# Graph attention on one core: keys fetched in three parts, query blocks stored in two parts, rows in two buffers

## The chip, the cores and the metric

The kernel runs on 1 core of a Trainium2 chip. The metric is device microseconds of one execution; a profiled execution gives the trace from which all rows below come. The five engines are named as in the profile: PE (TensorE), DVE (VectorE), ACT (ScalarE), POOL (GpSimd) and SP (SyncE, which here does nothing but issue transfers). "SPq" is SP's own queue of instructions, worked off strictly in order.

## What is computed

One layer of graph attention with five relation types, on 3125 nodes of 128 features and 100000 edges that are sorted by destination.

```python
def _fused_forward(node_embeddings, W_Q, W_K, W_V, attn_bias, out_proj_w, out_proj_b, ln_gamma, ln_beta, edge_index, edge_types):
    src, dst = (edge_index[0], edge_index[1])
    x_src = node_embeddings[src]
    x_dst = node_embeddings[dst]
    for r in range(R):                                   # 5 relations, 8 heads of 16
        mask = edge_types == r
        q = jnp.einsum('eh,khd->ekd', x_dst, W_Q[r])
        k = jnp.einsum('eh,khd->ekd', x_src, W_K[r])
        v = jnp.einsum('eh,khd->ekd', x_src, W_V[r])
        logits = (q * k).sum(-1) / scale + attn_bias[r][None, :]
        ... softmax over the edges of one destination, relation and head ...
        out = out + jax.ops.segment_sum(attn[:, :, None] * v, dst, num_segments=n)
    out = out.reshape(n, HIDDEN) @ out_proj_w.T + out_proj_b
    h = out + node_embeddings
    ... layer norm with ln_gamma, ln_beta ...
x = _layernorm(x + _L0_gnn_ref(x, edge_index, edge_type_5, ...), axis=-1)
```

## The kernel before

**Tiles and steps.** The 100000 edges are cut into 196 groups (`NGR`) of 512 (`GE`), each of four tiles (`T`) of 128 edges; 782 tiles (`NTILE`) hold edges. A step handles three groups (`G3`); `STEPS` puts the one left over into the first step, so there are 66 steps (`NST`): one of one group and 65 of three.

**Preamble.** For each of 25 blocks of 128 nodes, `table` (L472) multiplies the turned block with all key and value weights and stores a table row per node and relation in HBM, `kv_d` (L488). Between the blocks, the dictionary `side` (L650) places small pieces of work: loading indices, `keys_a/b/c`, `begins` (L404), masks, checks that the input has the expected form. `begins` takes the first destination of every tile from `fr`, which was loaded from HBM one element at a time, and makes from it `first`, `first15` (the row in `q_d` at which a tile's queries begin) and `gap`; `lr` holds the last destination of every group, loaded in the same way. On POOL, 60 gathers (`EARLY`, L355) fetch source rows of x into `xg` for the tiles that are treated below as early. The first four blocks' queries go to HBM as `q_d`, each query in three bf16 parts (L675).

**Gathers.** `gather(k)` (L796) fetches, on POOL, one tile per indirect transfer (L801) from `kv_d` into one of four slots of step k, three steps ahead of its use (`AHEAD`). A step in the steady part has 12 tiles; for 60 steps (`early_at`) one of them is not gathered but computed on PE from `xg` (`early_turn` L976, `early_rows` L985).

**What SP issues.** `fetch_rows(k)` (L712) loads for each of the step's 12 tiles the 120 query rows that its edges can need: for every four tiles one register load (L687), and for each tile one transfer of 30 KB from `q_d` (L717). `fetch_keys(k)` (L698) loads the step's keys, broadcast to 120 partitions, as one transfer of 360 KB. `fetch_masks(k)` (L846, transfer L850) loads the segment masks for the scans, `store_z` (L1222) stores finished output blocks. `store_q` (L842, transfer L675) stores one block of queries, 480 KB, into `q_d`; a block comes every third step or so, made in two halves in successive steps (`queries`, `first_part`, `remainder`, `second_part`, `third_part`). A transfer that reads `q_d` waits on SP until the last store into `q_d` has landed, and a store into `q_d` waits until the row loads issued before it have landed.

**The loop** (L1270), written out by hand; the order on each engine is the order of the calls. In step k: `products` and `logits` (query times key, summed by head, DVE), `turn_logits` (PE), `norm` and `relations` of step k-2, `spread_q(k+1)` (PE: one-hot times rows puts the right query beside each edge), `third_part` and `store_q`, `weigh(k-1)`, `gather(k+3)`, the two `scans` (DVE, L1002 and L1005: segment maxima both ways, they need the mask), `less_max`, `exps`, `spot(k+2)` (DVE: one-hot from the keys, L707), `turn_exps`, node-block work, and at the end:

```python
    def take(k):                                          # L1258
        if k + 3 < NST:
            fetch_keys(k + 3)
            fetch_rows(k + 3)
        if k + 2 < NST:
            fetch_masks(k + 2)
```

The keys have one buffer (`bufs=1`, so the transfer of step k+3 waits for `spot(k+2)`), the rows three, the masks two. After the loop, L1371 to L1406 finish the last three node blocks (`begun` and the two after it).

Of the kernel before, what the change touches and what calls it, by code (L numbers as in the profile page):

```python
# [9 lines left out]
F32 = mybir.dt.float32  # L10
BF16 = mybir.dt.bfloat16
# [36 lines left out]
STEPS = [NGR % G3] + [G3] * (NGR // G3)  # L48
# [21 lines left out]
ROUND, OFROUND, ROUNDS = 21, 20, 3  # L70
# [70 lines left out]
def windowed_path(  # L141
# [15 lines left out]
    def keep(name, shape, dt=F32):  # L157
        return const.tile(shape, dt, name=name)
# [6 lines left out]
    first15 = keep("first15", [1, NGR * T], I32)  # L165
# [40 lines left out]
    fr = load.tile([1, NGR * T], I32, name="fr")  # L206
    nc.vector.memset(fr[:, NTILE:], 0)
# [12 lines left out]

    early_src = load_early(nc.sync, "early_src", src)
# [49 lines left out]
    lr = load.tile([1, NGR], I32, name="lr")  # L271

    with nc.allow_non_contiguous_dma(reason="one element of each group"):
        for t, n, step, at in ((fr, NTILE, P, 0), (lr, NGR - 1, GE, GE - 1)):
            nc.scalar.dma_start(
                t[:, :n],
                bass.AP(tensor=dst.tensor, offset=dst.offset + at, ap=[[step * n, 1], [step, n], [1, 1]]),
            )
# [10 lines left out]
    nc.sync.dma_start(lr[:, NGR - 1 :], dst[E - 1 : E].rearrange("(o g) -> o g", o=1))  # L289
# [61 lines left out]
    busy(6)  # L351
    nc.vector.tensor_copy(xi, early_turned_up("early_src", early_src))
    busy(12)
    for e in range(EARLY):
        nc.gpsimd.indirect_dma_start(  # L355
            out=xg[:, e, :], out_offset=None, in_=x[:, :],
            in_offset=bass.IndirectOffsetOnAxis(ap=xi[:, e : e + 1], axis=0),
        )
# [45 lines left out]
    def begins():  # L404
        nc.vector.tensor_copy(frf, fr[:, ::T])
        nc.vector.tensor_copy(first, fr[:, ::T])
        nc.vector.tensor_scalar_mul(first15, fr, float(R * 3))
        fp = pps.tile([P, NGR], F32, name="fp", tag="tr", bufs=2)
        nc.tensor.matmul(fp, ones[0:1, :], frf, start=True, stop=True)
        firsts = load.tile([P, NGR], F32, name="firsts")  # L410
        nc.vector.tensor_copy(firsts, fp)
# [177 lines left out]
    lrf = load.tile([1, 2, NGR], F32, name="lrf")  # L589

    def wide_ends():
        nc.vector.tensor_copy(lrf[:, 0, :], lr)
# [20 lines left out]
    def short_tiles():  # L613
        spans = load.tile([HG, 2, T], F32, name="spans")
        nc.vector.tensor_tensor(
            spans, dst_r[:, :, P - 1 :: P], dst_r[:, :, ::P], op=ALU.subtract
        )
        nc.vector.tensor_scalar(
            spans, spans, float(QN - 1), None, op0=ALU.is_gt, op1=ALU.add,
            accum_out=vio[:HG, 6:7],  # L620
        )
        last = load.tile([1, 1], F32, name="last")
        nc.vector.tensor_tensor(
            last, lr[:, NGR - 1 :], fr[:, NTILE - 1 : NTILE], op=ALU.subtract
        )
        nc.vector.tensor_scalar(
            vio[0:1, 7:8], last, float(QN - 1), None, op0=ALU.is_gt
        )
# [17 lines left out]
    def late_x():  # L646
# [14 lines left out]
        10: [lambda: along(kvrow, 1, put_idx), begins],  # L661
        11: [keys_b],
        12: [sorted_rows, short_tiles],
# [22 lines left out]
    def starts(table, a, b, engine):  # L686
        _, at = nc.values_load_multi_w_load_instructions(  # L687
            table[0:1, a:b],
            engines=[engine],
            min_val=0,  # L690
            max_val=(N - 1) * (R * 3 if table is first15 else 1),
            skip_runtime_bounds_check_because="destinations are nodes",
        )
        return at
# [3 lines left out]
    def fetch_keys(k):  # L698
        n = B0[k + 1] - B0[k]
        live["kt", k] = kt = ahead.tile([3 * QR, TB * P], BF16, name="kt", bufs=1)  # L700
        keys = key_d.rearrange("g e -> (g e)")[B0[k] * P : B0[k + 1] * P]
        nc.sync.dma_start(kt[:, : n * P], keys.partition_broadcast(3 * QR))
# [9 lines left out]
    def fetch_rows(k):  # L712
        live["qw", k] = qw = ahead.tile([3 * QR, TB, H], BF16, name="qw", bufs=3)
        for a in range(B0[k], B0[k + 1], T):
            b = min(a + T, B0[k + 1])
            for j, f in enumerate(starts(first15, a, b, SPE)):
                nc.sync.dma_start(qw[:, a + j - B0[k], :], q_d[bass.ds(f, 3 * QR), :])  # L717
# [124 lines left out]
    def store_q(b):  # L842
        live.pop(("xT", b))
        store_rows(b, live.pop(("q3", b)))
# [82 lines left out]
    def closed_lanes(k):  # L927
        n, lg, lx = len(groups(k)), live.pop(("lg", k)), live["lx", k]
        into = lx.rearrange("p (u j) r k -> p j u r k", u=T)
        a, m = max(B0[k], 1), lg.shape[1]  # L930
        if m == T * n:
            closed(into[:, 1 : n + 1], lg, a)
        else:
            closed(into[:, 1:n], lg[:, : T * (n - 1)], a)
            closed(into[:, n : n + 1, : T - 1], lg[:, T * (n - 1) :], a + T * (n - 1))
            nc.vector.memset(lx[:SEG, (T - 1) * (G3 + 1) + n], 0.0)
# [297 lines left out]
    begun = max(b for b in range(NT) if done_at[b] < NST)  # L1234
    block_at = {k: b for b, k in done_at.items() if b < begun}
# [20 lines left out]
    fetch_rows(2)  # L1256

    def take(k):  # L1258
        if k + 3 < NST:
            fetch_keys(k + 3)  # L1260
            fetch_rows(k + 3)
        if k + 2 < NST:
            fetch_masks(k + 2)
# [6 lines left out]
    for k in range(NST):  # L1270
        new, old = k >= 1, k >= 2
        q0, (q, c0, c1), (q1, d0, _) = q_at.get(k), half(k), half(k - 1)
# [19 lines left out]
        if k == NST - 2:  # L1292
            places(G0[k + 1])
        elif k == NST - 1:
            place_next()
            place_g.append(G0[k] + 1)
# [14 lines left out]
        if q1 is not None:  # L1311
            third_part(q1, d0)
            if d0:
                store_q(q1)
# [10 lines left out]
        if k == NST - 1:  # L1325
            place_next()
        sum_next()
        scans(k)
        if k == done_at[begun]:
            project(begun)  # L1330
# [9 lines left out]
        if k < NST - 1:  # L1340
            place_next()
        if k == NST - 1:
            places(G0[k] + 2)
# [5 lines left out]
        if k == NST - 1:  # L1349
            for b in range(NT - len(ends), NT):  # L1350
                lifted(b)
            for b in range(begun, NT):
                shifted(b)
            residual(begun)
# [10 lines left out]
        if k < NST - 1:  # L1365
            weights(k)
        take(k)
# [4 lines left out]
    rest = [begun, begun + 1, begun + 2]  # L1372
    g = list(groups(k))
    assert rest[-1] == NT - 1 and done_at[begun - 1] < k - 1 and done_at[begun] < k
    assert full_at(rest[1]) < G0[k] and len(g) == G3
# [3 lines left out]
    weights(k)  # L1379
# [7 lines left out]
    norms(begun)  # L1387
    store_z(begun - 1)
    sums(g[1])
    project(rest[1])  # L1390
    residual(rest[1])
    roots(rest[1], last=True)
    sums(g[2])
    norm(k)
    relations(k, room[:, 2 * GE :])
    by_node(k)
    norms(rest[1])
    store_z(begun)
    project(rest[2])
    residual(rest[2])  # L1400
    roots(rest[2], last=True)
    norms(rest[2])
    store_z(rest[1])
    roots(NT, 1, 2, last=True)
    norms(NT)
    store_z(rest[2])  # L1406
# [507 lines left out]
```

## Time and profile before

| | |
|---|---|
| median of 3 runs | 1048.62 us (1045.79 to 1054.4) |
| profiled execution, own time | 1046.48 us |
| its span (first to last instruction) | 1044.2 us |
| busy: PE, DVE, POOL, ACT | 895.8, 883.0, 755.3, 718.6 us |
| mean granted TensorE clock | 0.922 |
| DMA | 192.83 MB, mean 185 GB/s |

The own time is 2.3 us over the span, for what lies before the first and after the last instruction. "Busy" of POOL leaves out what it needs between two gathers, and SP does not appear among the busy engines at all: issuing transfers, loading registers and waiting are not counted as busy. SP's rows are to be had from the timeline of its queue and from the table of its waits.

### The profile page before, as it was taken

What the parts mean: (1) busy time and instruction counts of PE and PEld (TensorE: products, weight loads), DVE (VectorE), ACT (ScalarE), POOL (GpSimd) and SP (SyncE); (2) the same over time, 40 slices, a digit from 0 to 9 for tenths busy, and PEclk for the clock granted to TensorE, in tenths of its full rate; (3) what the DMA queues carried; (4) which work ended last, traced back from release to release, by engine and by line L of the source; (5) the groups of instructions that cost most, each with busy time, mean ns of one, the idle gap of its engine ahead of it and who ended that gap; (6) DMA issues with size and microseconds to landing.
All of it is one profiled execution on the core that took longest, in us unless ns stands there. A gap on an engine that the chain in (4) does not pass through costs nothing.

```text
span 1044.2 us, 19181 instructions
## 1 busy us (share of the span) xinstructions
PE 895.8 (86%) x5371; PEld 660.7 (63%) x5371; DVE 883.0 (85%) x1383; ACT 718.6 (69%) x1936; POOL 755.3 (72%) x795
## 2 busy tenths in 40 slices
PE   6995589998999898889889988979989898979874
PEld 3553357776766676667667666757666666666653
DVE  2675479998998898999898998989989799979974
ACT  1444258886887677778677877768877787867562
POOL 6776777777777777777777777777777777777730
PEclk8997589998999898999899998989999899999786
DMA  6997667767677677777777777676777777767720
GB/s 157 353 331 258 172 172 185 180 179 184 175 194 190 177 191 181 187 175 182 190 180 190 191 180 174 181 187 186 187 193 180 189 182 196 176 177 179 171 64 13
DMA packets 176735, 192.83 MB, mean 185 GB/s; under 512 B 122398, under 2 KB 137640, under 8 KB 176498
## 3 DMA queue, kind: packets, MB, share of 16 engines
q0 software_dynamic: 36640, 98.65, 37.4%
q1 hardware_dynamic: 138190, 91.94, 31.9%
q10 hardware_dynamic: 1788, 0.92, 0.4%
q8 instruction: 45, 0.74, 0.3%
q14 instruction: 72, 0.59, 0.2%
HBM read 161.00 MB, written 30.40 MB: 183 GB/s over the span
## 4 chain that ended last, share of the span: by engine, by line
PE 30%; DVE 19%; DMA 13%; SPq 12%; POOL 10%; issue 9%; ACT 5%; ACTq 1%; DVEq 0%; POOLq 0%
SPq L717 8%; POOL kv_late L801 6%; PE qe L990 6%; DMA mk<-msk_d 5%; PE pr L479 5%; PE both L1075 5%; POOL kv_early L801 4%; SPq L687 4%; DVE lt L1002 4%; DVE lt L1005 3%; PE lt L979 3%; PE mid L1027 3%; DMA kv_early<-kv_d,idx 2%; DVE lg L921 2%; DMA q_d<-q 2%
## 5 line engine op out<-in xcount | busy, mean ns | idle before, releaser
L801 POOL DMA_INDIRECT kv_early<-kv_d,idx x368 | 353.9, 962 | 117.7 <-issue 105.4
L801 POOL DMA_INDIRECT kv_late<-kv_d,idx x354 | 339.3, 959 | 107.9 <-issue 102.7
L1075 PE MATMUL both<-wv,at 128*125 128x136 f32 x1544 | 282.5, 309 | 33.9 <-ACT at L1059 26.4
L1075 PEld LDWEIGHTS both<-wv,at 128*125 128x125 f32 x1544 | 218.3, 197 | 104.7 <-issue 49.4
L1056 ACT ACTIVATE at<-wide_at,nkey 128x125 f32<-128x125 f32 x772 | 243.8, 389 | 0.0
L990 PE MATMUL qe<-wkv,xr 128*128 128x256 f32 x600 | 148.9, 398 | 11.8 <-DVE kv_early L883 8.7
L1002 DVE TENSOR_TENSOR_SCAN lt<-mk,lt 120x640 f32<-120x640 bf16 (+1 forms) x66 | 98.5, 1492 | 42.0 <-DMA mk<-msk_d 25.3
L990 PEld LDWEIGHTS qe<-wkv,xr 128*128 128x128 f32 x600 | 115.2, 200 | 29.4 <-ACT diag L974 6.9
L1059 ACT ACTIVATE at<-at 128x500 f32<-128x500 f32 x193 | 119.6, 620 | 6.1
L1027 PE MATMUL mid<-gather_heads,ls 120*128 120x24 f32 (+1 forms) x528 | 73.7, 278 | 47.8 <-ACT xTq L816 29.5
L1020 ACT ACTIVATE ls<-ls 120x512 f32<-120x512 f32 (+1 forms) x66 | 41.6, 630 | 93.7 <-DVE ls L1012 91.9
L1027 PEld LDWEIGHTS mid<-gather_heads,ls 120*128 120x128 f32 (+1 forms) x528 | 69.1, 204 | 57.7 <-ACT xTq L816 34.4
L1005 DVE TENSOR_TENSOR_SCAN lt<-mk,lt 120x640 f32<-120x640 bf16 (+1 forms) x66 | 98.7, 1495 | 2.3
L979 PE MATMUL lt<-diag,xg 128*128 128x512 f32 x240 | 90.2, 504 | 0.0
L1070 PE MATMUL both<-wv,over 128*5 128x136 f32 x384 | 78.9, 289 | 0.0
L355 POOL DMA_INDIRECT xg<-in_x,xi x60 | 59.2, 987 | 21.2 <-issue 18.0
L883 DVE TENSOR_TENSOR kv_early<-kv_early,qe 128x128 f32<-128x128 f32 (+3 forms) x51 | 60.7, 1191 | 11.6 <-DMA kv_early<-kv_d,idx 10.9
L883 DVE TENSOR_TENSOR kv_late<-kv_late,qe 128x128 f32<-128x128 f32 (+2 forms) x48 | 58.4, 1216 | 13.5 <-DMA kv_late<-kv_d,idx 8.3
L952 PE MATMUL lt<-ident,lx 128*120 128x128 f32 (+2 forms) x396 | 56.9, 284 | 13.8 <-DVE both L1092 10.1
L979 PEld LDWEIGHTS lt<-diag,xg 128*128 128x128 f32 x240 | 45.7, 211 | 33.7 <-issue 33.7
L952 PEld LDWEIGHTS lt<-ident,lx 128*120 128x120 f32 (+2 forms) x396 | 41.3, 140 | 40.5 <-issue 32.3
L864 PE MATMUL qe<-qw,hot 120*128 120x128 bf16 x784 | 59.2, 225 | 9.0 <-DMA qw<-q_d 9.0
(200 smaller groups left out, 1405.2 us busy)
## 6 DMA issues: line engine op xcount, KB each, us to landing
qw<-q_d SPq DMA_DIRECT2D x784, 30.0 KB
kt<-key_d SPq DMA_DIRECT2D x64, 360.0 KB
kv_d<-kvs SPq DMA_DIRECT2D x24, 640.0 KB
q_d<-q SPq DMA_DIRECT2D x25, 480.0 KB
mk<-msk_d SPq DMA_DIRECT2D x65, 150.2 KB
kv_early<-kv_d,idx POOLq DMA_INDIRECT x368
kv_late<-kv_d,idx POOLq DMA_INDIRECT x354
out<-z SPq DMA_DIRECT2D x24, 64.0 KB
```

Of the source, the lines that this page charges most:

```text
L717: nc.sync.dma_start(qw[:, a + j - B0[k], :], q_d[bass.ds(f, 3 * QR), :])
L801: nc.gpsimd.indirect_dma_start(out=kv[:, at, :], out_offset=None, in_=kv_d[:, :], in_offset=bass.IndirectOffsetOnAxis(ap=idx[:, q % T, q / ...
L883: nc.vector.tensor_tensor(kv[:, c0:c1, :H], kv[:, c0:c1, :H], qe[:, n:m], op=ALU.mult)
L952: nc.tensor.transpose(live["lt", k][: n * LANES, c : c + w], live["lx", k][p : p + w, j : j + n].rearrange("p g r k -> p (g r k)"), ident[ ...
L979: nc.tensor.matmul(lt[:, c0:c1], xg[:, e, :], at[:, c0:c1], start=True, stop=True)
L990: nc.tensor.matmul(rows, xr[:, r * P : (r + 1) * P], wkv[:, r].rearrange("h s c -> h (s c)"), start=(r == 0), stop=(r == R - 1),)
L1002: nc.vector.tensor_tensor_scan(lt, mk[:n, :WIDE], lt, -BIG, op0=ALU.add, op1=ALU.max)
L1005: nc.vector.tensor_tensor_scan(lt[:, ::-1], mk[:n, WIDE:0:-1], lt[:, ::-1], -BIG, op0=ALU.add, op1=ALU.max)
L1027: nc.tensor.matmul(ex.rearrange("p (i t) k -> p t i k", t=T)[:, t], ls[: n * LANES, t * P : (t + 1) * P], gather_heads[: n * LANES, :n], s ...
L1056: nc.scalar.activation(at[:, t, :], row_at[:, :WR], AF.Abs, bias=nkey[:, t, g : g + 1], scale=1.0)
L1059: nc.scalar.activation(at[:, :n], at[:, :n], AF.Relu, bias=1.0, scale=-1.0)
L1075: nc.tensor.matmul(pp[:WR], at[:, t, :], wv[:, T * i + t, :], start=(t == 0), stop=(t == end))
```

## The change

In the loop, `take` is gone. At the head of step k, SP is given, for i = 0, 1, 2, the rows of the i-th four tiles of step k+2, then (at i = 2) the masks of step k+1, then the i-th part of the keys of step k+3. The key buffers become two, the row buffers two. Each half of a query block is stored as soon as it is complete. The early tiles are 62 in two rounds of 31 (steps 2 to 63). The first destinations come out of `dst_w`, which is loaded anyway, by way of two PE products, and the element-wise loads of `fr` and `lr` are gone; the first three gathers into `xg` take their indices from a small transfer, `direct`. The steps are 64 of three groups and two of two, and the end is written anew with idle matmuls (`busy_end`) and an activation table loaded ahead.

```diff
-STEPS = [NGR % G3] + [G3] * (NGR // G3)
+STEPS = [G3] * (NGR // G3 - 1) + [2, 2]
...
-ROUND, OFROUND, ROUNDS = 21, 20, 3
+ROUND, OFROUND, ROUNDS = 31, 31, 2
+DIRECT = 3
...
-    fr = load.tile([1, NGR * T], I32, name="fr")
...
-    early_src = load_early(nc.sync, "early_src", src)
+    direct = load.tile([P, DIRECT], I32, name="direct")
+        nc.sync.dma_start(
+            direct,
+            bass.AP(
+                tensor=src.tensor, offset=src.offset + T * G0[EARLY0 + 1] * P,
+                ap=[[1, P], [T * G3 * P, DIRECT], [1, 1]],
+            ),
+        )
...
     load_weights(nc.scalar, wn[: R * HEADS, :], w_k)
+    early_src = load_early(nc.sync, "early_src", src)
     load_weights(nc.sync, wn[R * HEADS :, :], w_v)
-    load_x(0, 2)
-    load_x(2, 4, nc.scalar)
+    load_x(0, 2, nc.scalar)
+    load_x(2, 4)
...
-        for t, n, step, at in ((fr, NTILE, P, 0), (lr, NGR - 1, GE, GE - 1)):
-            nc.scalar.dma_start(
-                t[:, :n],
-                bass.AP(tensor=dst.tensor, offset=dst.offset + at, ap=[[step * n, 1], [step, n], [1, 1]]),
-            )
...
-    def begins():
-        nc.vector.tensor_copy(frf, fr[:, ::T])
...
+    def edges_of():
+        nc.vector.tensor_copy(edge[:, :, :T], dst_r[:, :, ::P])
+        nc.vector.tensor_copy(edge[:, :, T:], dst_r[:, :, GE - 1 :])
...
+    def begins(s):
+        diag = load.tile([HG, HG, T + 1], F32, name="diag")
+        nc.vector.tensor_tensor(
+            diag,
+            ident[:HG, :HG, None].to_broadcast([HG, HG, T + 1]),
+            edge[:, s, None, :].to_broadcast([HG, HG, T + 1]),
+            op=ALU.mult,
+        )
+        fp = pps.tile([P, HG, T + 1], F32, name="fp", tag="wp", bufs=2)
+        nc.tensor.matmul(
+            fp.rearrange("p g t -> p (g t)"), ones[:HG, :], diag.rearrange("p g t -> p (g t)"),
+            start=True, stop=True,
+        )
...
+        nc.vector.tensor_copy(firsts[:, a:e], fp[:, :n, 0])
...
-    def fetch_keys(k):
+    def fetch_keys(k, parts=range(G3)):
         n = B0[k + 1] - B0[k]
-        live["kt", k] = kt = ahead.tile([3 * QR, TB * P], BF16, name="kt", bufs=1)
-        keys = key_d.rearrange("g e -> (g e)")[B0[k] * P : B0[k + 1] * P]
-        nc.sync.dma_start(kt[:, : n * P], keys.partition_broadcast(3 * QR))
+        if 0 in parts:
+            live["kt", k] = ahead.tile([3 * QR, TB * P], BF16, name="kt", bufs=2)
+        for i in parts:
+            a, b = T * i, n if i == G3 - 1 else min(T * i + T, n)
+            if a < b:
+                keys = key_d.rearrange("g e -> (g e)")[(B0[k] + a) * P : (B0[k] + b) * P]
+                nc.sync.dma_start(
+                    live["kt", k][:, a * P : b * P], keys.partition_broadcast(3 * QR)
+                )
...
-    def fetch_rows(k):
-        live["qw", k] = qw = ahead.tile([3 * QR, TB, H], BF16, name="qw", bufs=3)
+    def fetch_rows(k, parts=range(G3)):
+        if 0 in parts:
+            live["qw", k] = ahead.tile([3 * QR, TB, H], BF16, name="qw", bufs=2)
...
-    def store_q(b):
-        live.pop(("xT", b))
-        store_rows(b, live.pop(("q3", b)))
+    def store_q(b, c0, c1):
+        q3 = live["q3", b]
+        nc.sync.dma_start(
+            q_d[b * P * R * 3 : (b + 1) * P * R * 3, :].rearrange("(p c) h -> p (c h)", c=3 * R)[
+                :, 3 * c0 * H : 3 * c1 * H
+            ],
+            q3[:, c0:c1].rearrange("p r s h -> p (r s h)"),
+        )
...
-    fetch_rows(2)
...
-    def take(k):
...
+        for i in range(G3):
+            if k + 2 < NST:
+                fetch_rows(k + 2, [i])
+            if k + 1 < NST and k and i == G3 - 1:
+                fetch_masks(k + 1)
+            if k + 3 < NST:
+                fetch_keys(k + 3, [i])
         if q1 is not None:
             second_part(q1, d0)
...
             third_part(q1, d0)
-            if d0:
-                store_q(q1)
+            store_q(q1, d0, d1)
...
-        take(k)
...
-    weights(k)
-    roots(begun, last=True)
-    for i in range(G3):
-        weigh(k, i, i + 1)
     norm(k - 1)
-    sums(g[0])
     relations(k - 1, room[:, GE:])
+    busy_end(5)
+    weigh(k)
     by_node(k - 1)
+    nc.scalar.preload_act_table_set("sqrt_and_others")
+    sums(g)
+    sums(g + 1)
+    project(b)
+    norm(k)
+    busy_end(4)
...
```

In the built program SP issues in the loop's steady part, per step, four row loads, a key part, four row loads, a key part, four row loads, the masks, a key part, and in two of about three steps half a query block; the next instruction after that half is the register load for the next step's rows, and the first of these rows waits for the half to have landed. In all there are 784 row loads before and after, 66 key transfers before and 191 after, 21 stores of query blocks in the loop before and 42 halves after.

More of the change, by code (lines that the diff above doesn't have):

```diff
@@ L686, in starts @@
     def starts(table, a, b, engine):
+        if table is first15:
+            if a < HG * T < b:
+                return starts(table, a, HG * T, engine) + starts(table, HG * T, b, engine)
+            s = int(a >= HG * T)
+            table, a, b = first15[32 * s :], a - s * HG * T, b - s * HG * T
         _, at = nc.values_load_multi_w_load_instructions(
@@ L1233, in windowed_path @@
         done_at[b] = max(done_at[b], done_at[b - 1] + 1)
[L1234 to L1235 removed]
+    block_at = {k: b for b, k in done_at.items() if k < NST - 1}
     q_from = {}
@@ L1371, in windowed_path @@
     k = NST - 1
[L1372 to L1375, printed above, removed]
+    b, g = NT - 2, G0[k]
+    assert max(block_at.values()) == b - 1 and AT[full_at(b)][0] == k - 1 and STEPS[k] == 2
     room = ps.tile([P, T * G3, H], F32, name="qe").rearrange("p n h -> p (n h)")
@@ L1378, in windowed_path, with busy_end @@
     live["both", k] = room[:, : G3 * (PW + HEADS + WN)]
-    weights(k)
-    roots(begun, last=True)
-    for i in range(G3):
-        weigh(k, i, i + 1)
+    none = ps.tile([P, T * GE // 2], F32, name="lt")
+    idle = ahead.tile([3 * QR, TB * P], BF16, name="hot", bufs=1)
+    nc.vector.memset(idle[:, : GE // 2], 0.0)
+    def busy_end(n):
+        for _ in range(n):
+            nc.tensor.matmul(
+                none[:, : GE // 2], idle[:, :P], idle[:, : GE // 2], start=True, stop=True
+            )
     norm(k - 1)
-    sums(g[0])
     relations(k - 1, room[:, GE:])
+    busy_end(5)
+    weigh(k)
     by_node(k - 1)
[L1387 to L1393, printed above, removed]
+    nc.scalar.preload_act_table_set("sqrt_and_others")
+    sums(g)
+    sums(g + 1)
+    project(b)
     norm(k)
+    busy_end(4)
     relations(k, room[:, 2 * GE :])
+    busy_end(4)
+    residual(b)
+    roots(b, last=True)
     by_node(k)
[L1397 to L1403, printed above, removed]
+    norms(b)
+    store_z(b - 1)
+    project(b + 1)
+    residual(b + 1)
+    roots(b + 1, last=True)
+    norms(b + 1)
+    store_z(b)
     roots(NT, 1, 2, last=True)
     norms(NT)
-    store_z(rest[2])
+    store_z(b + 1)
     ctx.close()
```

97 lines of the change are left out of this document (49 added, 48 removed).

## The prediction

> **What bounds the kernel now.** I read the page's costliest groups first, for the engine whose idle time has no releaser; then the timeline of POOL; then, because SP's work is in no busy figure, the timeline of SP's queue and its waits; last the chain that ended last, for landings.
>
> ```profile
> L801 POOL DMA_INDIRECT kv_early<-kv_d,idx x368 | 353.9, 962 | 117.7 <-issue 105.4
> L801 POOL DMA_INDIRECT kv_late<-kv_d,idx x354 | 339.3, 959 | 107.9 <-issue 102.7
> ...
> 83.32 0.94 POOL L355 DMA_INDIRECT xg<-in_x,xi  x1 [0.30 <-issue]
> 90.09 0.95 POOL L801 DMA_INDIRECT kv_early<-kv_d,idx  x1 [5.83 <-DVE q L739]
> ...
> 1002.06 0.95 POOL L801 DMA_INDIRECT kv_early<-kv_d,idx  x1 [0.30 <-issue]
> ```
>
> POOL's 722 gathers run from 90.09 to 1003.01, which is 1.264 us each; busy plus idle in the two rows is also 1.264 (918.8 less the 5.83 before the first). An ordinary gather is 0.95 and 0.30 of issue. So POOL never stops: 11 gathers of a step are 13.9 us. It is one bound. SP is the other, and hardly looser:
>
> ```profile
> 547.64 0.72 SPq L850 DMA_DIRECT2D mk<-msk_d  x1
> 548.46 0.41 SPq L1226 DMA_DIRECT2D out<-z  x1
> 549.29 0.36 SPq L675 DMA_DIRECT2D q_d<-q  x1
> 549.70 2.92 SPq L702 DMA_DIRECT2D kt<-key_d  x1
> 555.70 8.98 SPq L717 DMA_DIRECT2D qw<-q_d  x12
> 564.73 0.75 SPq L850 DMA_DIRECT2D mk<-msk_d  x1
> 565.59 0.42 SPq L702 DMA_DIRECT2D kt<-key_d  x1
> 567.45 9.01 SPq L717 DMA_DIRECT2D qw<-q_d  x12
> 576.51 0.73 SPq L850 DMA_DIRECT2D mk<-msk_d  x1
> 577.34 0.42 SPq L702 DMA_DIRECT2D kt<-key_d  x1
> ```
>
> From mask to mask a step without a store takes 11.78 us of SP (564.73 to 576.51), the one with a store 17.09 (547.64 to 564.73): the block's store is issued at 549.29 and the next rows only at 555.70, 6.41 later. The next rows show how much of the loop SP fills, and who makes it wait:
>
> ```profile
> L717 SPq DMA_DIRECT2D qw<-q_d x784: 329/330/1654, 100.5 to 987.9; - x196
> L687 SPq TENSOR_LOAD <-first x197: 525/1138/2757, 97.2 to 985.3; - x197
> L702 SPq DMA_DIRECT2D kt<-key_d x66: 338/417/2915, 73.5 to 978.3; - x66
> ...
> SPq L717 <- DMA q_d<-q: 59.7, 22, 3.9
> SPq L702 <- DVE near L1193: 6.0, 4, 3.8
> SPq L702 <- DVE xn L1156: 4.7, 3, 1.8
> SPq L702 <- DVE lx L895: 4.5, 5, 2.5
> SPq L702 <- DVE hot L707: 3.7, 3, 2.2
> ```
>
> The row loads stretch over 887.4 us. Waits for other engines are 18.9 us in the four DVE rows and some 29 with the smaller rows of that view; the rest, 858 us, is SP's own issuing and its waits for landings. SP is thus full to 97% beside POOL's 100%, and DVE now and then pays for it:
>
> ```profile
> DVE lt L1002 <- DMA mk<-msk_d: 25.3, 12, 7.2
> ```
>
> These late masks stand behind the waiting SP. They cost no end time, since POOL does not stop for them.
>
> **The change, part by part: POOL and the preamble.** Two tiles fewer are gathered: 720 instead of 722, 2 x 1.264 = 2.5 us less. The start of the gathers hangs on the node table, and this on the first weights:
>
> ```profile
> 2.15 7.02 DMA wn<-in_L_gnn_W_V
> 9.20 7.32 ACTq L275
> ...
> 17.66 3.80 PE pr L479 x4
> ...
> 47.69 0.59 PE fp L409 x2
> ```
>
> The weights land at 9.2, then ACT sits 7.32 us in the issue of the element-wise load of `lr` while its copies of the weights wait, so PE begins the table at 17.66. Without it the table could begin about 4.5 us earlier. Against that stand two products of 495 columns for one of 196 (0.59 us at 196, so about 1.5 each, 2.4 more) with two DVE products ahead of them in PE's order, and `direct`, whose 384 single elements go ahead of the weights on SP; nothing shows its price, between nothing and the 7.32 for the 195 elements of `lr`. I take 3 us of gain at the gathers' and rows' start, bounds 0 and 7. POOL's 62 gathers into `xg` instead of 60 end about 2.5 later than 84.26, still ahead of 87. POOL alone would then end at 90.1 - 3 + 720 x 1.264 = 997.
>
> **SP.** What `take` held goes to the head of the steps: the same 784 row loads, the same 196 register loads, the same masks. Added are 125 key transfers (191 for 66) and 21 stores of halves (42 for 21).
> - A key part has 120 rows of 1 KB. Neighbours: 0.33 us for 120 rows of 256 bytes, 0.417 for 120 of 3 KB. I take 0.42 and 0.05 between instructions, 0.47; bounds 0.38 and 0.80 (the mask's 0.75 and the gap). 125 x 0.47 = 59.
> - A whole store costs 17.09 - 11.78 = 5.3 us beyond a step without one, in 21 steps 111. It is the landing, less what SP does meanwhile (a key transfer, 0.47, and a register load with gaps, 1.26), plus 0.65 for issue and waits ahead of it. After the change a half does the same twice: behind it comes no key transfer, only the register load, and then a row load that waits until the half has landed; everything else on SP (masks, keys, later `store_z`) is queued behind. So a half costs landing + 0.1 - 1.26 + 0.65.
>
> How long does a half take to land? No row shows 288 or 192 KB; these are the neighbours, the last in a quiet queue:
>
> ```profile
> 326.23 6.75 DMA q_d<-q
> 495.24 6.02 DMA mk<-msk_d
> ...
> 113.66 2.62 DMA mk<-msk_d
> 96.83 3.41 DMA q_d<-q
> ```
>
> In the loop 480 KB take up to 6.75 us, and a mask of 150 KB still 6.02 (of 50 KB in the quiet queue 2.62). So size hardly sets it, the crowd does, and masks and a key part go in right ahead of each half. I take 5.6, bounds 3.41 and 6.75. A half then costs 5.1, 42 of them 214, which is 103 more than 111. (By 3.41: 122, 11 more; by 6.75: 262, 151 more.)
>
> The Trainium skill, page "DMA: Bandwidth & Descriptors", section "Anatomy of one DMA — SWDGE (gpsimd) path", puts a transfer at about 2.0 us and its bytes over 436 GB/s; an estimate by that page is 2.66 and 2.45 us for the halves, and a half would cost 2.0 us, all of them 86, less than the 111 of whole stores. The quiet 3.41 for 480 KB agrees with it (3.13), the 6.75 does not.
>
> SP's sum: 858 + 59 + 103 = 1020 us. The 29 us of waits for others go, since SP is now late everywhere. The last row load is issued at 97.5 + 1020 = 1117.5 instead of 987.9.
>
> **The rest of the loop.** Two row buffers: rows of step k+2 wait for `spread_q(k)` on PE, done half a step before SP comes there, so no price while SP is late; if SP were early, the wait would cost SP only idle time. Two key buffers: the wait for `spot` goes (in the 29). The two extra early tiles put PE and ACT work into steps that wait anyhow. With SP at 15.6 us a step, POOL will stop for slots that `weigh` frees late; DVE and PE (90% busy) will wait for rows and masks.
>
> **The end.** The masks of step 64 follow the last rows.
>
> ```profile
> 1003.50 1.49 DVE L1002 TENSOR_TENSOR_SCAN lt<-mk,lt 120x640 f32<-120x640 bf16 x1
> 1013.19 1.74 DVE L1043 TENSOR_TENSOR wv<-kv_early,mid 128x1536 f32<-128x1536 f32 x1
> 1014.91 1.50 DVE L1002 TENSOR_TENSOR_SCAN lt<-mk,lt 120x640 f32<-120x640 bf16 x1
> 1021.81 1.28 ACT L1171 ACT_TABLE_LOAD   x1
> ```
>
> Masks land some 4 us after the last row (1121.5), the scan of step 64 starts, and that of step 65 follows 11.4 us later before; with two groups a third goes from `weigh` and the two like it (1.74 each, 1.8 in all), so 9.5. From the last scan to the end were 29.3; one group less in `weigh` and `sums` and the table load ahead (1.28) save about 2.8, the idle matmuls keep to PE: 26.5. End of span 1121.5 + 9.5 + 26.5 = 1157.5; the profiled execution's own time lay 2.3 above its span (1046.48 to 1044.2), and 2.1 below the median 1048.62, which I leave out. About 1158, with other mean sizes 1150 to 1165; I say 1155.
>
> **The rivals.**
> - *Halves land quickly, POOL stays the bound.* If a half costs 2.05 us or less (landing 2.6), SP's sum is 892 and its last row comes at 990, in time for POOL's end at 997. Then the end is 997 + 41.2 - 2.8 + 2.3 = 1038, faster. For it: POOL's unbroken rows, and the late masks would vanish. Against: no landing in the loop's chain is under 5 us. By the estimate from the Trainium skill above, the halves' total gives this case.
> - *SP bound, light queue.* With fewer transfers in flight landings fall towards 3.41: sum 858 + 59 + 11 = 928, last row 1025, end about 1066. For it: the 17.09 step has keys of 360 KB that now go in parts. Against: the mask's 6.02.
> - *SP bound, dearer.* Keys at the mask's price (100 for 59) and landings of 6.75 (151 for 103): 1155 + 41 + 48 = 1244; either alone about 1200.
> - *The additions cancel.* With landings of 3.0 a half costs 2.5, 42 of them 105: sum 858 + 59 - 6 = 911, last row 1008.5, end about 1049, within 1% of 1048.62 (1% is about what a measurement of this kernel can tell from no change). For it: the quiet 3.41; against: as above.
>
> **How the numbers follow.** Forecast, SP as the bound with halves near the whole store's landing: 0.64, from 1085 to 1210. Light queue 0.13, dearer 0.08, quick halves 0.10 (of which 0.08 under 1038 and 0.02 just above), cancelled 0.05. That is faster 0.08, same 0.07, slower 0.85. The range reaches from 1062, the light queue's end, to 1212 and leaves out the quick halves, the cancelled case and half of the dearer one.
>
> **What would show it.** Right: SP's queue with 42 waits of rows for `q_d` stores, of 3 us and more each, over 120 us in sum; mask to mask near 12.7 us without a half and near 17.5 with one; gaps on POOL before gathers; DVE waiting for masks or PE for rows in most steps; last row load after 1080. Wrong: POOL still without gaps and the last row load before 1000, or half-store landings under 3 us; then SP was not the bound, and the time is near 1038.

## The result, and the profile after

The changed kernel takes 1164.97 us, median of four runs (1162.39 to 1171.45), beside 1049.61 for the kernel before (1045.79 to 1054.4): the ratio is 1.1106, with a 95% interval of 1.1037 to 1.1175. The profiled execution took 1171.45, the slowest of the four, and its span is 1169.4. The prediction said 1155, range 1062 to 1212.

The costliest groups of the page after, the rows that answer to POOL's rows and to the late masks of before (busy, mean ns of one | idle before them and what ended most of it):

```profile
L844 POOL DMA_INDIRECT kv_early<-kv_d,idx x367 | 355.0, 967 | 168.1 <-issue 103.9
L844 POOL DMA_INDIRECT kv_late<-kv_d,idx x353 | 339.9, 963 | 166.2 <-issue 101.9
L1054 DVE TENSOR_TENSOR_SCAN lt<-mk,lt 120x640 f32<-120x640 bf16 (+1 forms) x66 | 98.6, 1494 | 139.2 <-DMA mk<-msk_d 125.5
```

A gather is as long as before, and there are two fewer. But POOL's idle time beside its own issue has gone from 17.5 us (225.6 less 208.1) to 128.5 (334.3 less 205.8). DVE now waits 125.5 us for masks where it waited 25.3. POOL is no longer the bound. The table of waits says for whom each of them stands (us in all, times, longest):

```profile
POOL kv_late L844 <- DVE wv L1095: 62.8, 25, 6.5
POOL kv_early L844 <- DVE wv L1095: 52.2, 18, 5.7
...
SPq L758 <- DMA q_d<-q: 116.8, 43, 4.4
...
SPq L887 <- DMA qw<-q_d: 24.4, 43, 1.9
```

POOL waits for slots that `weigh` (L1095) frees late, DVE for masks (125.5 us in 43 waits), and the masks stand in SP's queue behind rows that wait for the halves of query blocks: 43 waits, one for each half and one ahead of the loop. The chain that ended last, by engine and by line, names the same pieces:

```profile
DMA 26%; SPq 24%; PE 23%; DVE 16%; issue 7%; ACT 2%; POOL 1%; DVEq 0%; ACTq 0%
SPq L758 14%; DMA mk<-msk_d 10%; DMA q_d<-q 9%; SPq L719 7%; PE pr L508 4%; PE both L1127 4%; PE lt L1031 4%; DMA qw<-q_d 4%; DVE lt L1054 3%; DVE lt L1057 3%; PE mid L1079 3%; PE qe L1042 3%; SPq L738 2%; DVE lg L972 1%; DVE kv_early L934 1%
```

What a step costs SP is read in the timeline of its queue (start, us, instruction; L758 are rows, L901 masks, L738 key parts, L887 a half's store):

```profile
532.74 0.75 SPq L901 DMA_DIRECT2D mk<-msk_d  x1
533.54 0.46 SPq L738 DMA_DIRECT2D kt<-key_d  x1
534.76 0.37 SPq L887 DMA_DIRECT2D q_d<-q  x1
541.12 1.97 SPq L758 DMA_DIRECT2D qw<-q_d  x4
543.13 0.41 SPq L738 DMA_DIRECT2D kt<-key_d  x1
544.91 1.91 SPq L758 DMA_DIRECT2D qw<-q_d  x4
546.88 0.40 SPq L738 DMA_DIRECT2D kt<-key_d  x1
548.63 1.90 SPq L758 DMA_DIRECT2D qw<-q_d  x4
550.59 0.74 SPq L901 DMA_DIRECT2D mk<-msk_d  x1
...
563.04 0.75 SPq L901 DMA_DIRECT2D mk<-msk_d  x1
```

From mask to mask the step with a half takes 17.85 us here (532.74 to 550.59) and the next, without one, 12.45 (to 563.04). Between the half's store and the next row lie 6.36 us. Over the 61 steps in the middle of the run the same rows give these means (a step with or without a store, from mask to mask; from a store to the first row behind it; the rows' stretch from the first to the last of 784):

| | step without | step with (count) | store to row | rows' stretch | span |
|---|---|---|---|---|---|
| before | 12.01 | 16.97 (21) | 6.24 | 887.4 | 1044.2 |
| after | 12.77 | 17.01 (42) | 5.13 | 1011.9 | 1169.4 |

The span is 125.2 us longer, and 124.5 of it lie in the rows' stretch: 100.5 to 987.9 before, and after (minimum, median and longest of one in ns, first and last start):

```profile
L758 SPq DMA_DIRECT2D qw<-q_d x784: 329/330/1648, 106.0 to 1117.9; - x196
```

In the table of SP's waits, taken from 116 to 988 us before and from 125 to 1118 after, the waits for landings rose from 68.8 to 142.5 us. Those for other engines fell from 30.8 to 14.4. So neither DVE nor PE sets SP's pace, although the mean granted TensorE clock was 0.860 here and 0.922 before, and PE was busy for 972.0 us instead of 895.8. The trace has 196 key transfers, 130 more than before, and not the 191 of the section on the change.

### The profile page after: what moved, and what is told of

Same layout as the page of the kernel before. It is cut to its first block, busy times and chain, and to the rows that moved or that the text cites. A ratio compares the mean times of both kernels' runs of the same rounds, so it can differ in the third digit from the quotient of the medians.

```text
span 1169.4 us, 19517 instructions
## 1 busy us (share of the span) xinstructions
PE 972.0 (83%) x5408; PEld 713.0 (61%) x5408; DVE 887.9 (76%) x1390; ACT 727.9 (62%) x1949; POOL 759.5 (65%) x795
## 4 chain that ended last, share of the span: by engine, by line
DMA 26%; SPq 24%; PE 23%; DVE 16%; issue 7%; ACT 2%; POOL 1%; DVEq 0%; ACTq 0%
SPq L758 14%; DMA mk<-msk_d 10%; DMA q_d<-q 9%; SPq L719 7%; PE pr L508 4%; PE both L1127 4%; PE lt L1031 4%; DMA qw<-q_d 4%; DVE lt L1054 3%; DVE lt L1057 3%; PE mid L1079 3%; PE qe L1042 3%; SPq L738 2%; DVE lg L972 1%; DVE kv_early L934 1%
## 5 line engine op out<-in xcount | busy, mean ns | idle before, releaser
L1127 PE MATMUL both<-wv,at 128*125 128x136 f32 x1552 | 305.9, 326 | 36.3 <-ACT at L1111 29.3
L1127 PEld LDWEIGHTS both<-wv,at 128*125 128x125 f32 x1552 | 238.4, 213 | 112.2 <-issue 51.7
L1054 DVE TENSOR_TENSOR_SCAN lt<-mk,lt 120x640 f32<-120x640 bf16 (+1 forms) x66 | 98.6, 1494 | 139.2 <-DMA mk<-msk_d 125.5
L1079 PE MATMUL mid<-gather_heads,ls 120*128 120x24 f32 (+1 forms) x528 | 91.3, 316 | 107.9 <-DVE h L1216 57.6
L1079 PEld LDWEIGHTS mid<-gather_heads,ls 120*128 120x128 f32 (+1 forms) x528 | 85.5, 246 | 120.0 <-ACT ls L1072 89.7
L1042 PEld LDWEIGHTS qe<-wkv,xr 128*128 128x128 f32 x620 | 120.4, 203 | 17.6 <-issue 1.7
L1031 PE MATMUL lt<-diag,xg 128*128 128x512 f32 x248 | 122.1, 634 | 0.0
L1031 PEld LDWEIGHTS lt<-diag,xg 128*128 128x128 f32 x248 | 60.6, 270 | 48.8 <-issue 48.8
L1035 ACT COPY xr<-lt 128x640 f32<-128x640 f32 x62 | 42.9, 692 | 67.2 <-PE lt L1031 66.3
L508 PE MATMUL pr<-wkv,xT 128*128 128x512 f32 x150 | 62.9, 566 | 1.1 <-ACT kvs L512 0.8
L972 DVE TENSOR_REDUCE lg<-kv_early 128x8 f32<-128x128 f32 (+3 forms) x51 | 60.6, 1189 | 0.6
```

The lines of the kernel that those rows point to most:

```text
L508: nc.tensor.matmul(pr[:, : c1 - c0, :], xT, wf[:, c0:c1, :], start=True, stop=True)
L1031: nc.tensor.matmul(lt[:, c0:c1], xg[:, e, :], at[:, c0:c1], start=True, stop=True)
L1042: nc.tensor.matmul(rows, xr[:, r * P : (r + 1) * P], wkv[:, r].rearrange("h s c -> h (s c)"), start=(r == 0), stop=(r == R - 1),)
L1054: nc.vector.tensor_tensor_scan(lt, mk[:n, :WIDE], lt, -BIG, op0=ALU.add, op1=ALU.max)
L1079: nc.tensor.matmul(ex.rearrange("p (i t) k -> p t i k", t=T)[:, t], ls[: n * LANES, t * P : (t + 1) * P], gather_heads[: n * LANES, :n], s ...
L1127: nc.tensor.matmul(pp[:WR], at[:, t, :], wv[:, T * i + t, :], start=(t == 0), stop=(t == end))
```

## Experiments

Three theories stood against one another. **S**: SP's queue sets the time, by the sum of its issues and of its waits for landings. **L**: the rows come late because they have two buffers. **C**: more transfers crowd the DMA engines. L was worded in the expectations as a lead of two steps for three; in the order of the program the place is in fact the same, since the end of step k, where `take` asked for rows of step k+3, is the head of step k+1. Only the buffers differ.

**Whole stores.**

```diff
-            store_q(q1, d0, d1)
+            if d1 == R:
+                store_q(q1, 0, R)
```

> The changed kernel, but each query block is stored whole, once, when its second half is complete (21 stores of 480 KB for 42 halves). Theory S (SP's queue sets the time; its sum of issues and of waits for landings is the time): a step with a half takes 16.9 us of SP from mask to mask and one without 12.5, so a half costs 4.4 and 42 of them 185; a whole store with only a register load behind it costs 5.8 (5.3 before, when a key transfer of 0.47 covered part), 21 of them 122. 63 us less: about 1102. Theory L (the rows come too late because they have two buffers and a lead of two steps instead of three): nothing changes, 1155 to 1175. Theory C (the additional transfers crowd the DMA engines, bytes and queue do not matter by themselves): 21 transfers of 1100 fewer, within 1% of 1165.

Measured: 1100.81 us, ratio 1.0489 (1.0429 to 1.0548): S to within 2 us, and out of the ranges of L and C. 64 us of the loss are the halves. The same 30 KB rows, two buffers and key parts now take

```profile
L758 SPq DMA_DIRECT2D qw<-q_d x784: 329/330/1900, 105.8 to 1054.1; - x196
...
SPq L758 <- DMA q_d<-q: 72.8, 22, 4.4
```

948.3 us, with 22 waits for stores in place of 43. A whole store lands more slowly than a half (6.32 us from store to row for 5.13), but there are half as many.

**Keys in one transfer.**

```diff
-            if k + 3 < NST:
-                fetch_keys(k + 3, [i])
+            if k + 3 < NST and i == G3 - 1:
+                fetch_keys(k + 3)          # one transfer of 360 KB
```

> The changed kernel, but each step's keys come as one transfer of 360 KB, at the place of the third part. Theory S: two issues of 0.46 us fewer in 64 steps, 59 us less, about 1106; halves wait for their landing as long as before. Theory L: 1155 to 1175. Theory C: same bytes in 128 transfers fewer, 1150 to 1165.

Measured: 1156.02 us, ratio 1.1015 (1.0956 to 1.1074), 9 us less and not 59. S failed here by 50 us. The number lies in the ranges of L and C, but the run with whole stores had left both. The waits and the queue show what S had left out:

```profile
SPq L752 <- DMA q_d<-q: 171.6, 43, 6.0
...
550.08 0.76 SPq L895 DMA_DIRECT2D mk<-msk_d  x1
550.94 0.42 SPq L734 DMA_DIRECT2D kt<-key_d  x1
551.69 0.38 SPq L881 DMA_DIRECT2D q_d<-q  x1
552.12 0.44 SPq L1272 DMA_DIRECT2D out<-z  x1
558.65 8.52 SPq L752 DMA_DIRECT2D qw<-q_d  x12
567.22 0.75 SPq L895 DMA_DIRECT2D mk<-msk_d  x1
568.02 0.46 SPq L734 DMA_DIRECT2D kt<-key_d  x1
569.13 0.37 SPq L881 DMA_DIRECT2D q_d<-q  x1
```

The issues did become cheaper: a step without a store takes 11.60 us of SP instead of 12.77. But the half is now issued just behind a key transfer of 360 KB instead of one of 120, and from store to row lie 6.58 us on average instead of 5.13: 42 x 1.45 = 61 of the 61 x 1.17 = 71 us that the issues saved. A step with a half is no shorter than before (17.23 us, 17.01 after the change). The waits for halves grew by 54.8 (171.6 for 116.8). So a landing is not a fixed price: it grows with what SP put into its queue ahead of the store (call this **Q**; it was found here, after S had failed; the next two runs bear on it). The Trainium skill, page "DMA: Bandwidth & Descriptors", section "Queues, rings and completion order", says that each DMA engine takes a queue's descriptors in order and that the completion signal follows every earlier write of that engine; the two numbers agree with it.

**Both.**

> The changed kernel with whole stores and with keys in one transfer; two row buffers, the lead of two steps, the new order, the start and the end stay as changed. Theory S: 122 us less would be 1043, but POOL's unbroken gathers bound it: 95.9 + 720 x 1.264 + 41.2 - 2.8 + 2.3 = 1047; 1045 to 1060, near the kernel before. Theory L: the lead is still two steps, so 1150 to 1175. Theory C: the DMA load is that of before, near 1049 too.

Measured: 1074.26 us, ratio 1.0262 (1.0197 to 1.0326). All three expectations failed. The rows' stretch is 917.3 us, with 11.95 for a step without a store and 18.40 for one with. It misses 1047 for the reason of Q: a whole store right behind 360 KB of keys takes 7.56 us to the next row, against 6.24 in the kernel before, where the same 360 KB are issued right behind the store. Bytes ahead of a store thus count for more than bytes behind it, which move at the same time. The sizes agree too. Beside the run with whole stores alone, a step without a store lost 0.93 us (12.88 to 11.95), 57 in 61 steps, and the way from store to row grew by 1.24 (6.32 to 7.56), 26 for 21 stores. That leaves 31, and the rows' stretch fell by 31.0 (948.3 to 917.3).

**Only the order changed.** All transfers of the changed kernel are kept; masks and key parts go ahead of the rows, so that they lie between a half's store and the row that waits for it.

```diff
-        for i in range(G3):
-            ... rows k + 2 part i; masks k + 1 at the last; keys k + 3 part i
+        if k + 1 < NST and k:
+            fetch_masks(k + 1)
+        if k + 3 < NST:
+            fetch_keys(k + 3)              # three parts
+        if k + 2 < NST:
+            fetch_rows(k + 2)
```

> The changed kernel with every transfer kept, halves and key parts too; only their order at the head of a step is another: first the masks of step k+1, then the three key parts of step k+3, then the twelve rows of step k+2. Behind a half SP then has 0.8 + 3 x 0.46 = 2.2 us of work before the first row that waits for it. Theory S: 2.2 of a half's 4.4 us are covered, 42 times, 92 us less: about 1073. Theory L: rows are issued no earlier, 1155 to 1175, or a little less since masks come earlier. Theory C: the same transfers, and masks and keys now share the DMA engines with the half, so that it lands later by as much as is covered: 1150 to 1175.

Measured: 1101.1 us, ratio 1.049 (1.0433 to 1.0547), 64 us less with not one transfer fewer. That rules out C as the cause of those 64 us, and bears out S; its size was too high by 28.

```profile
SPq L887 <- DMA qw<-q_d: 64.3, 65, 2.4
...
568.71 0.38 SPq L887 DMA_DIRECT2D q_d<-q  x1
569.15 0.76 SPq L901 DMA_DIRECT2D mk<-msk_d  x1
569.95 1.43 SPq L738 DMA_DIRECT2D kt<-key_d  x3
572.83 1.95 SPq L758 DMA_DIRECT2D qw<-q_d  x4
```

Behind the half SP works without a pause: keys end at 571.38, the register load and its gaps take the usual 1.4, and the rows come 4.12 after the store. Rows wait for a store once in the whole run, for 2.3 us, and that is ahead of the loop. So with nothing but landed rows ahead of it each half had landed when SP came to the row, 4.44 us after the store on average (4.04 to 5.86). What is given back stands in the first line: the store itself must wait until the rows ahead of it have landed, 64.3 us in all instead of 24.4, because masks and keys no longer lie between them. A half costs 15.33 - 12.98 = 2.35 us of SP in place of 4.24.

**Masks and keys from another engine's queue.** The edit writes `nc.scalar.dma_start` for `nc.sync.dma_start` in `fetch_keys` and `fetch_masks`.

> The changed kernel with every transfer kept in its place and size, halves and key parts too; the masks and the key parts are issued by ACT instead of SP. Theory S (SP's queue sets the time): a step of SP without a half, 12.77 us, loses 3 x 0.46 + 0.8 and takes 10.6; one with a half 14.8 instead of 17.01; 19 and 42 of them are 823 us, less than the 61 x 13.9 = 848 that POOL needs for the same steps. POOL is the bound again: 95.9 + 720 x 1.264 + 41.2 - 2.8 + 2.3 = 1047, and up to 1065 if ACT, which issues 140 us more, is late with something. Theory C (what costs is the number of transfers on the DMA engines) or L (rows two steps ahead in two buffers come too late): the same transfers with the same lead, 1150 to 1175. This holds beside a kernel before of about 1049 on the same chip; beside one of about 1680 the engines stand still for other reasons, and nothing follows for the queue.

Measured: 1177.37 us, ratio 1.1285 (1.1217 to 1.1353): the expectation of S failed. Its bound of 1065 left out what ACT's queue does. ACT's timeline:

```profile
529.59 0.56 ACTq L738 DMA_DIRECT2D kt<-key_d  x1
530.03 0.22 ACT L1089 COPY wv<-mid 128x96 f32<-128x96 f32 x1
530.19 0.32 ACTq L738 DMA_DIRECT2D kt<-key_d  x1
530.55 0.72 ACTq L901 DMA_DIRECT2D mk<-msk_d  x1
533.33 0.33 ACTq L738 DMA_DIRECT2D kt<-key_d  x1
533.70 0.69 ACT L1035 COPY xr<-lt 128x640 f32<-128x640 f32 x1 [3.45 <-DMA kt<-key_d]
```

SP's queue at the same time:

```profile
529.76 0.38 SPq L887 DMA_DIRECT2D q_d<-q  x1
533.43 1.95 SPq L758 DMA_DIRECT2D qw<-q_d  x4
```

The last key part is issued at 533.33, 2.06 us after the mask's issue ended, and only then does ACT copy `xr`. The releaser `kt` in that line misleads. By the operands in the trace, the transfers of SP and ACT take turns on eight semaphores, and one is issued only when the transfer that used its semaphore last has landed. This key part has the semaphore of the half that SP stored at 529.76, which landed at 533.30; SP's own next row goes out at the same moment. Ahead of keys and masks ACT stood for some 99 us in all until a transfer had landed, and 95 of them were for transfers that SP had issued: rows, halves and output blocks (43 waits). PE waits 135.1 us for `xr`. So the wait was not removed but moved to an engine that has work of its own. SP in turn stands 111.2 us waiting for output blocks to store, and the chain that ended last is spread over DMA (26%), PE (21%), DVE (15%), ACT and SP's queue (13% each). This run neither confirms nor refutes that SP's issues alone made the loss; queues that share no semaphore were not tried.

**The order of before, with the rest of the change.** Whole stores, one key transfer behind the store, the start of before; the two row buffers, 62 early tiles, short last steps and the new end stay.

```diff
-            live["kt", k] = ahead.tile(..., name="kt", bufs=2)     # three parts
+        live["kt", k] = kt = ahead.tile(..., name="kt", bufs=1)    # one transfer
...
-            store_q(q1, d0, d1)
+            if d1 == R:
+                store_q(q1, 0, R)
...
         weights(k)
+        if k + 3 < NST:
+            fetch_keys(k + 3)
```

> All of the change but four things: whole stores for halves, one key transfer of 360 KB in one buffer for three parts in two, issued behind the place of the store (so SP's order is that of the kernel before: store, keys, rows, masks), and the start of the kernel before. What stays of the change: two row buffers for three, 62 early tiles, short last steps, the new end. Theory S with what the runs showed of landings (behind a store nothing but its own bytes and a mask is in the queue, and the keys cover part of the landing): SP is as full as in the kernel before, POOL runs without a break from 90.1 and ends 720 x 1.264 later at 1000.2; with 41.2 - 2.8 to the end and 2.3 around the span 1041, 1036 to 1048, so equal to the kernel before or up to 1% faster. Theory L (two row buffers make the rows late, a part of what the change costs): 1060 to 1090, since the buffers are those of the change.

Measured: 1047.47 us beside 1047.05, ratio 1.0006 (0.9975 to 1.0037). Its rows:

```profile
L722 SPq DMA_DIRECT2D qw<-q_d x784: 329/330/1550, 98.6 to 990.4; - x196
...
L808 POOL DMA_INDIRECT kv_early<-kv_d,idx x367 | 352.1, 959 | 114.6 <-issue 103.3
L808 POOL DMA_INDIRECT kv_late<-kv_d,idx x353 | 339.9, 963 | 107.8 <-issue 103.8
```

891.8 us for the rows (887.4 before), POOL unbroken again, and the last gather ends at 1000.8 where S had 1000.2. L falls: two row buffers cost nothing that shows. The whole loss of the change thus lies in the four things undone here. Undone one after another, the parts gave back 64 us (the halves, 1164.97 to 1100.81), 27 (the key parts on top of them, to 1074.26) and 27 (the keys' place and buffer and the start on top of both, to 1047.47). Two gathers fewer and the new end together bring nothing: from the last gather to the end of the span are 45.8 us (1000.8 to 1046.6), where before had 41.2. No version tried beats the kernel before.

**Six runs that tell little.** Halves alone and key parts alone on the kernel before were run, and key parts issued behind the half's store and the ACT queue were run twice, where the kernel before itself took 1671 to 1693 us, on two chips, one of which gave 1048 for it at another time.

> The kernel before with one part of the change alone: each half of a query block stored as soon as it is complete (42 stores for 21); keys whole, three row buffers, old order. Theory S: a half costs here what it costs after the change, 4.4 us, less the key transfer that SP issues behind it in this order (0.47), 3.9; 42 of them 165 against 111 for whole stores, 54 more on a queue that had 29 us of room: the rows end 25 to 54 later and SP takes the bound over: 1064 to 1095, say 1078. Theory C (what costs is the number of transfers in flight): 21 more of 1100, within 1% of 1048.

> The kernel before with another part alone: each step's keys in three transfers of 120 KB, one behind the other, at the old place ahead of the rows and in the one buffer. Theory S: 130 issues of 0.46 more are 60 us; in the 21 steps with a store the two more of each lie in the time in which the store lands (0.92 x 21 = 19); 41 remain on a queue that had 29 us of room: 1050 to 1080, say 1060. Theory C: 130 transfers more on the DMA engines with the same bytes, within 1% of 1048.

> The changed kernel with every transfer kept; rows and masks stay at the head of a step, the three key parts are issued behind the place of the half's store instead of ahead of it. Theory S with the landing as it is: 1.4 us of a half's landing is covered by issues, but the store, which waits until the rows ahead of it have landed, waits some 0.6 longer: 0.8 x 42 = 34 us less, about 1130. Theory Q (a store lands only behind the bytes that SP put into the same queue ahead of it, as one transfer of 360 KB ahead made the halves' waits 55 us longer in all than three of 120 KB): without 120 to 360 KB of keys just ahead the landing is itself up to 1 us shorter: about 1090. Theory C: 1150 to 1175.

> The changed kernel with every transfer kept in its place and size; the masks and the key parts are issued by ACT instead of SP, the rows and halves stay on SP. Theory S: SP loses 64 x (1.38 + 0.8) = 140 us of issues; its sum of 1012 becomes 872, the last row comes near 980, ahead of POOL's end at 95.9 + 720 x 1.264 = 1006; POOL is the bound again: 1006 + 41.2 - 2.8 + 2.3 = 1047, and up to 1065 if ACT, which issues 140 us more, is late with something. Theory C or L: the same transfers with the same lead, 1150 to 1175.

Measured there: halves alone 1675.28, ratio 0.9991 (0.9933 to 1.005); keys alone 1685.57, 1.0112 (1.0032 to 1.0192); keys behind the store 1728.62, 1.0366 (1.0287 to 1.0445), and in a second run 1759.94 (1726.1 to 1766.39); ACT's queue 1757.42, 1.0538 (1.0458 to 1.0618), and again 1792.91, 1.0618 (1.0546 to 1.069). POOL's rows in the run with the halves alone show that another limit ruled:

```profile
L801 POOL DMA_INDIRECT kv_early<-kv_d,idx x368 | 352.6, 958 | 457.0 <-DVE wv L1051 281.8
L801 POOL DMA_INDIRECT kv_late<-kv_d,idx x354 | 339.1, 958 | 377.5 <-DVE wv L1051 266.2
```

A gather is as short as ever, but POOL idles 834.5 us, 548.0 of them until `weigh` frees a slot (`wv`). A bound by SP's queue is not seen under such a limit, so neither the 0.9991 nor the others speak for or against S. The two parts alone on the kernel before, and the keys behind the halves, stay untested where SP counts.

## Why the prediction was right, step by step

**SP as the bound: shown.** The signs named for it came: 43 waits of rows for `q_d` stores, 12.77 and 17.01 us from mask to mask (12.7 and 17.5 were named), POOL's gaps, DVE's 43 waits for masks, and a last row at 1117.9. The waits' sum was put at "over 120 us"; it was 116.8. "3 us and more each" was too much: the mean is 2.7 and the longest 4.4, because a half landed sooner than the 5.6 us that were put in.

**Halves, the term mis-sized most.** The prediction put a half at 5.1 us of SP from a landing of 5.6, 42 against 21 whole stores at +103. Measured: 17.01 - 12.77 = 4.24 for a half and 16.97 - 12.01 = 4.96 for a whole one, 42 x 4.24 - 21 x 4.96 = 74. From store to row are 5.13 us, so the landing is about 5.0. The step that failed is "size hardly sets it, the crowd does": a whole store in the same place takes 6.32, 1.2 more than a half, and 240 KB more of keys ahead take 1.45 more. Bytes do count, the store's own and those ahead of it. That also answers the estimate of 2.66 and 2.45 us from the Trainium skill, page "DMA: Bandwidth & Descriptors", section "Anatomy of one DMA — SWDGE (gpsimd) path": in this queue a half lands in about 5.0 behind 120 KB of keys and a mask, and had landed by 4.44 on average behind landed rows; no run shows one alone. That section of the Trainium skill is on transfers that GpSimd issues, while the halves go out from SP.

**Keys.** 125 parts at 0.47, 59 us, were predicted; there are 130, which by that price are 61. A step without a store rose by 0.76 us (12.01 to 12.77), which over 61 steps is 46. The parts themselves cost more: 0.93 a step by the two runs with whole stores (12.88 to 11.95) and 1.17 by the one-transfer run (12.77 to 11.60), 57 to 71. The net rise is smaller since SP's waits for other engines fell; the prediction let all 29 us of them go, and 16 went (30.8 to 14.4). The one-transfer run's time fell by 9 us only: taken alone the term cannot be had back, because the size of the transfer ahead of a store sets the store's landing. Small key parts cost issues and save landing.

**The sum.** 74 and 46 are 120 of the 124.5 by which the rows' stretch grew; 133 were predicted. That the last row, put at 1117.5, came at 1117.9 is luck: it is a start 8.5 us later than put (106.0 for 97.5) and a stretch 8.1 shorter (1011.9 for 1020). The end then took 11.5 longer than put, so the span came to 1169.4 instead of 1157.5; the median lies 6.5 us below this execution, which brings it nearer to the 1155.

- *The start* was to gain 3 us; the first rows came at 106.0 instead of 97.5. PE did begin the table 4.3 us earlier, at 13.39 instead of 17.66. But the two products for the first destinations cost their own time and the wait for DVE ahead of each, in the timeline of PE:

```profile
44.67 1.15 PE L425 MATMUL fp<-diag,ones 99*128 99x495 f32 x2 [1.78 <-DVE diag L418]
...
53.11 1.99 PE L425 MATMUL fp<-diag,ones 99*128 99x495 f32 x2 [3.42 <-DVE diag L418]
```

  Together 8.3 us, where the prediction had 2.4 more than before. ACT and DVE also wait longer for table stores to land, 5.2 us between 30 and 95 us instead of 2.4. The start varies from run to run too: the two runs with keys in one transfer have the same code ahead of the loop, and their first rows came at 101.5 and 105.1.
- *The end* from the last row was to take 40 us and took 51.5. The failing step is "the scan of step 64 starts" when its mask has landed. DVE was not there yet. In the windows from 1106 to 1119, 1119 to 1130 and 1130 to 1141 us DVE is busy all but a little:

```profile
1106.00:1119.00 13.00, 10.53 (x69) 8.18 (x70) 11.71 (x15) 7.97 (x23) 5.71 (x6) 0.87 0.51 120
1119.00:1130.00 11.00, 9.10 (x60) 6.51 (x60) 10.53 (x18) 8.76 (x28) 0.00 (x0) 0.89 0.07 20
1130.00:1141.00 11.00, 10.04 (x62) 7.79 (x62) 10.63 (x22) 8.14 (x24) 0.00 (x0) 0.80 0.03 8
```

  After the window's length stand the busy us of PE, PEld, DVE, ACT and POOL: DVE has 11.71 of 13, 10.53 of 11 and 10.63 of 11 us. Once the rows are out, SP limits no more and DVE does; the chain has the scan of step 64 at 1130.88 instead of 1121.5, which is 9.4 of the 11.5 us.

**The rivals.** Quick halves, the light queue and the cancelled case needed landings of 2.6, 3.41 and 3.0 us and fall by the 5.0 that a half took; the dearer one falls by that too (6.75 was its landing) and by a key part's issue of 0.41. One argument against quick halves was misread: that no landing in the loop's chain before is under 5 us is so for stores and masks, but rows stand there with 1.82 to 2.44.

## What to carry to other kernels

Count the in-order queue that issues the transfers as an engine: sum its issues and its waits for landings per step, and hold them against the engines that the profile calls busy. Where loads wait in such a queue for a store in it, one store cost less here than two halves (18.08 - 12.88 = 5.2 us of SP for 2 x 4.24), and large transfers belong behind the store, where their issue hides part of the landing, not ahead of it, where their bytes lengthen it. Before transfers go to another engine's queue, look at what each issue there will wait for.

## What the runs showed that was not expected

- A transfer of 360 KB ahead of a store, instead of 120 KB, lengthened its landing by 1.45 us on average, which used up 61 of 71 us of saved issues.
- ACT stood some 99 us ahead of its key and mask issues, nearly all of it for landings of transfers that SP had issued, because the two queues take turns on the same eight semaphores. The Trainium skill, page "DMA: Bandwidth & Descriptors", section "Issuing engines are not separate DMA queues", says that issuing from several engines saves only the time to initiate a transfer, usually small beside the transfer. Here that time and SP's waits were the bound, and moving part of it to ACT was still no gain.
- The same kernel before took 1048 us on one chip and 1693 on it at a later time. With the halves alone (1666.8 of span) the chain that ended last puts 28% to "another core or an unknown queue". DVE, ACT and POOL are busy for about as long as in the kernel before (889.5, 723.4 and 751.2 us), PE for longer (1068.8 us instead of 895.8, at a mean granted clock of 0.745). What held the engines there is open.
